# A four-head attention layer: its 65-column matmuls emitted as one burst per head, or queued and put one by one behind other matmuls

## The chip, the cores and the metric

The kernel runs on one core of a Trainium2 chip. The metric is the device time of one execution in microseconds (us), as the median of several runs. The five engines that matter are named as in the profile: PE (matmuls) with PEld (its weight loads), DVE (elementwise work and reductions), ACT (activations), POOL (here mostly indirect transfers) and SP (it issues the plain transfers). Each engine works through its own list of instructions in the order in which the program was built.

## The reference, cut to what matters

Four graph-attention layers are applied to 32 independent batch elements of 512 nodes x 256 features, each as `x = x + layer(relu(layernorm(x)))`. Layers 0 and 1 are single-head attention layers over the adjacency mask. Layer 2, the one that the change touches, has four heads of 64 features:

```python
Wh = (h @ W).reshape(B, N, 4, 64)
s_src = einsum('bnhd,hd->bnh', Wh, a_src); s_dst = einsum('bnhd,hd->bnh', Wh, a_dst)
e = leaky_relu(s_src[:, :, None, :] + s_dst[:, None, :, :], 0.2)
e = where(mask, e, -inf)                    # mask: 512 x 512 adjacency
alpha = softmax(e, axis=2)                  # per head, over the 512 sources j
h_out = einsum('bijh,bjhd->bihd', alpha, Wh)
return elu(h_out)
```

Layer 3 is an MLP with two attentions inside, one of them without a mask, which the kernel computes by sorting. Everything is fp32.

## The kernel before, in words

A row of 512 nodes is four blocks of 128 (`NT = 4`), so one batch element is a handful of 128-row tiles and all of its state stays on chip. `fast` (line 36) does the work; `general` (line 803) is a second version that runs only if a flag says that values left a safe range, and it isn't entered in the runs here.

**Streams and the planner.** Four streams (`NS = 4`, lines 760 to 786) each carry one batch element at a time through `layer0` to `layer3`. Every stage is a Python generator. When it yields, it gives a due time, and the loop at line 770 always resumes the stream whose due time is smallest. So the planner decides nothing at run time: its due times only decide the order in which the instructions of four batch elements are laid into each engine's list. `after_us(us)` (line 60) computes a due time as the stage's own start, plus `STRETCH` (2) times the matmul time that the stage has emitted so far, plus `SLOW` (1.5) times the latency that the stage names. Stream i starts `i * LEAD` planner microseconds late; `LEAD` is 75. Some instructions are tied to their place with `keep_in_program_order`.

**PSUM.** `bank()` (line 77) gives each stream two of the eight accumulator banks, in turn.

**Layer 2** (line 452). Four projections of 268 columns (lines 455 to 467) give a tile `v` that holds, for each node block and head, 64 scaled features, a column of scales (the softmax denominator's column) and two factors. The leaky ReLU of a sum, exponentiated, is written as a maximum of two products, so an attention weight needs a single VectorE instruction, `scalar_tensor_tensor` with max and then mult by the mask (line 353). It makes a 128 x 512 block: 128 sources j by all 512 targets. `weights` (line 343) makes the four blocks of a head into one tile of 128 x 4 x 512 fp32, tag `w`, four buffers. It needs the row of the other factor on all partitions. For head 0 it comes from four transposes into a PSUM bank (line 349), for heads 1 to 3 it goes out to DRAM (`rows_out`, line 362, L369) and comes back broadcast (`spread`, line 372, L375, two buffers, so the third one waits until head 1's weights are made).

For each head, `aggregate` (line 381) is called for the four target blocks t, and inside it runs over the four source blocks j: 16 matmuls of 128 x 128 weights and 65 moving columns (64 features and the denominator), which accumulate into one bank, t outermost and j innermost:

```python
for t in range(NT):
    aggregate(p[:, t * (D + 1):(t + 1) * (D + 1)], wt, t, lambda j: v[:, j, h, :D + 1])
```

All 16 are emitted in one piece, with nothing between them, and then come the reciprocal, the product into `ya` (lines 496 to 499), and after each second head the ELU and the addition to `x` (lines 500 to 506). `begin(h + 1)` makes the weights of the next head a head early. Four normalisations of pairs of blocks end the layer (lines 508 to 510).

The other layers' matmuls are longer: 257 moving columns in the single-head aggregations, 259 and 256 in projections, 512 in the MLPs (`linear_t`). All of them go through `matmul` (line 64, recorded as L66) and all transposes through `transpose` (L70).

**SP's list** holds, for one stage of the planner after another: the row out and the three spreads of a stream in layer 2 (L369, L375), the sorted values (L614, L615) and the table (L647, L648) of another stream in layer 3, stores of results (L716) and loads of inputs (L95).

Of the kernel before, what the change touches and what calls it, by code (L numbers as in the profile page):

```python
# [8 lines left out]

# [1 line left out]

# [6 lines left out]
FP = mybir.dt.float32  # L20
BF = mybir.dt.bfloat16
I32 = mybir.dt.int32
# [13 lines left out]
def fast(ctx, tc, flag, x, adj, w0, a0, w1, a1, w2, a2, mlp1_w, mlp1_b, mlp2_w, mlp2_b,  # L36
# [7 lines left out]
    NH = a2.shape[0]  # L44
    D = F // NH
    NS = 4
    LEAD = 75.0
    SLOW = 1.5
    STRETCH = 2.0

    const = ctx.enter_context(tc.tile_pool(name="const", bufs=1))
    work = ctx.enter_context(tc.tile_pool(name="work", bufs=2))
# [7 lines left out]
    def after_us(us):  # L60

        return begun[0] + STRETCH * spent[0] / CYCLES + SLOW * us

    def matmul(p, w, x, **flags):
        spent[0] += 4 * max(x.shape[-1], P)
        nc.tensor.matmul(p, w, x, **flags)  # L66

    def transpose(p, x, i, tied=False):
        spent[0] += 2 * P
        instruction = nc.tensor.transpose(p, x, i)  # L70
        if tied:
            tc.keep_in_program_order(instruction)

    active = set()
    banks = [0]

    def bank():

        own = [turn[0], *(i for i in range(NS) if i not in active and i != turn[0])]
        banks[0] += 1  # L80
        return psum.tile([P, N], FP, tag=f"b{own[banks[0] % len(own)]}", name="b", bufs=8 // NS)
# [68 lines left out]
    a0_sb = fetch_a(a0, "W0a")  # L150
    xts = {0: load_x(0)}
    W0, _ = fetched0 = fetch_w(w0, a0_sb, "W0")
    adj_sb = work.tile([P, NT, N], I32, tag="w", name="adj", bufs=4)
    nc.sync.dma_start(adj_sb, adj.rearrange("(t p) j -> p t j", p=P))
    for b in range(1, NS):
        xts[b] = load_x(b)
# [49 lines left out]

    def setup():

        own = work.tile([P, NT, N], FP, tag="w", name="own", bufs=4)
        nc.vector.tensor_scalar(own, adj_sb, 0.0, None, op0=OP.is_gt)  # L210
        nc.gpsimd.affine_select(
            out=own, in_=own, pattern=[[P, NT], [-1, N]], base=0, channel_multiplier=1,
            compare_op=OP.not_equal, fill=1.0,
        )
        tc.keep_in_program_order(nc.vector.tensor_reduce(differ[:, 0:1], adj_sb, AX.XY, OP.min))
        nc.vector.tensor_scalar(differ[:, 0:1], differ[:, 0:1], 0.0, None, op0=OP.is_lt)
        for j in range(NT):
            turn[0] = NS - 1 - j % (NS - 1)
            p = bank()
            for t in range(NT):  # L220
                transpose(p[:, t * P:(t + 1) * P], own[:, t, j * P:(j + 1) * P], ident, j + t == 0)
            nc.scalar.copy(maskT[:, j, :], p)
        turn[0] = NS - 1
        yield
        yield from finish_w(fetched1, 0.01)


        least = small([1], "rden")
        nc.vector.tensor_reduce(least, diag, AX.X, OP.min)
        nc.vector.tensor_scalar(differ[:, 1:2], least, 0.0, None, op0=OP.is_le)  # L230
        nc.vector.tensor_copy(W2[:, :, :, :D], raw2.rearrange("p k (h d) -> p k h d", d=D))
        nc.vector.tensor_scalar_mul(A2v[:, :, 1:2], A2v[:, :, 0:1], -0.8)
        nc.vector.tensor_scalar_mul(A2v[:, :, 2:3], A2v[:, :, 2:3], 0.8)
        for k in range(KF):
            project(W2[:, k, :, D:], lambda k, f: raw2[:, k, f * P:(f + 1) * P], k, A2)
            yield
        yield from finish_w(fetched3, 0.2)

        for tri, sign in ((before, 1), (after, -1)):
            nc.vector.memset(tri, 1.0)  # L240
            nc.gpsimd.affine_select(
                out=tri, in_=tri, pattern=[[sign, P]], base=0, channel_multiplier=-sign,
                compare_op=OP.is_gt, fill=0.0,
            )
        ties = work.tile([P, 2 * N - P], FP, tag="w", name="ties", bufs=4)
        nc.vector.memset(ties, TINY)
        nc.gpsimd.affine_select(
            out=ties, in_=ties, pattern=[[-1, 2 * N - P]], base=N - P, channel_multiplier=1,
            compare_op=OP.is_gt, fill=0.0,
        )  # L250
        nc.vector.tensor_copy(band, ties)
        yield
        yield from finish_w(fetched4, 0.2)
# [49 lines left out]
    def note(e):  # L303

        c = next(noted)
        nc.vector.tensor_reduce(seen[:, c:c + 1], e, AX.XY, OP.max)
# [33 lines left out]
            yield after_us(0.9 if f == ft - 1 else 0)  # L340
        return o

    def weights(r_col, t_col, masked=True, r=None):

        landed = r is not None
        if not landed:
            r = bank()
            for t in range(NT):
                transpose(r[:, t * P:(t + 1) * P], r_col(t).to_broadcast([P, P]), ident)
        wt = work.tile([P, NT, N], FP, tag="w", name="w", bufs=4)  # L350
        for j in range(NT):
            if masked:
                w = nc.vector.scalar_tensor_tensor(  # L353
                    wt[:, j, :], r, t_col(j), maskT[:, j, :], op0=OP.max, op1=OP.mult
                )
                if landed and j == 0:
                    tc.keep_in_program_order(w)
            else:
                nc.vector.tensor_scalar(wt[:, j, :], r, t_col(j), None, op0=OP.max)
        return wt  # L360

    def rows_out(cols, n):

        p = bank()
        transpose(p[:NT * n, :P], cols, ident)
        row = work.tile([P, P], FP, tag="row", name="row", bufs=1)[:NT * n, :]
        nc.scalar.copy(row, p[:NT * n, :P])
        row_d = dram.tile([n, N], FP, tag="row", name="row", bufs=4)
        nc.sync.dma_start(row_d.rearrange("n (t p) -> t n p", p=P), row)  # L369
        return row_d  # L370
# [9 lines left out]

    def aggregate(p, wt, t, rhs):
        for j in range(NT):
            matmul(p, wt[:, j, t * P:(t + 1) * P], rhs(j), start=(j == 0), stop=(j == NT - 1))

    def reciprocal(den):
        r = small([1], "rden") if len(den.shape) == 2 else small([NH, 1], "rden4")
# [65 lines left out]
    def layer2(xt, xn, rs, when):  # L452
        hT = yield from turned(xn, when)
        v = work.tile([P, NT, NH, CH], FP, tag="v", name="v2", bufs=4)
        for t in range(NT):
            ps = bank()
            for k in range(KF):
                matmul(
                    ps[:, :NH * CH], hT[:, k, t * P:(t + 1) * P], W2[:, k, :, :], start=(k == 0), stop=(k == KF - 1)
                )  # L460
            pv = ps[:, :NH * CH].rearrange("p (h c) -> p h c", c=CH)
            nc.scalar.activation(v[:, t, :, D:], pv[:, :, D:], AF.Exp, scale=rs[:, t:t + 1])
            nc.vector.scalar_tensor_tensor(  # L463
                v[:, t, :, :D], pv[:, :, :D], rs[:, t:t + 1], v[:, t, :, D:D + 1].to_broadcast([P, NH, D]),
                op0=OP.mult, op1=OP.mult,
            )
            yield after_us(0 if t + 1 < NT else 1)
        ya = work.tile([P, NT, F], FP, tag="y4", name="y4", bufs=1)
        wts = []

        def begin(h):
            wts.append(
                weights(
                    lambda t: v[:, t, h, D + 2:D + 3], lambda j: v[:, j, h, D + 1:D + 2], r=far[h]
                )
            )
            return after_us(3.2)

        row_d = rows_out(v[:, :, :, D + 2], NH)
        far = [spread(row_d[h, :]) if h else None for h in range(NH)]
        when = begin(0)
        note(v.rearrange("p t h c -> p (t h) c")[:, :, D:])
        yield after_us(3)
        for h in range(NH):
            last = when
            if h + 1 < NH:
                when = begin(h + 1)
            yield last  # L490
            wt = wts[h]
            p = bank()
            for t in range(NT):
                aggregate(p[:, t * (D + 1):(t + 1) * (D + 1)], wt, t, lambda j: v[:, j, h, :D + 1])
            pv = p[:, :NT * (D + 1)].rearrange("p (t c) -> p t c", c=D + 1)
            r = reciprocal(pv[:, :, D:])
            nc.vector.tensor_tensor(
                ya[:, :, h * D:(h + 1) * D], pv[:, :, :D], r.to_broadcast([P, NT, D]), op=OP.mult
            )
            if h % 2:  # L500
                c = slice((h - 1) * D, (h + 1) * D)
                y = ya[:, :, c]
                q = pair("q").rearrange("p a (b f) -> p (a b) f", f=2 * D)
                nc.scalar.activation(q, y, AF.Exp)  # L504
                nc.scalar.activation(y, y, AF.Relu)  # L505
                add_elu(xt[:, :, c], y, q)
            yield after_us(0)
        xn, rs = new_xn(), small([NT], "rs")
        for t0 in range(0, NT, 2):
            norm(xt, xn, rs, t0, False)  # L510
        yield after_us(7)
        return xn, rs, after_us(2)
# [720 lines left out]
```

## Time and profile before

| what | value |
|---|---|
| median of 3 runs | 2932.55 us (2931.43 to 2941.0) |
| profiled execution: its span | 2929.6 us (the page states no other time for it) |
| busy: PE / PEld / DVE / ACT / POOL | 98% / 80% / 76% / 52% / 17% of the span |
| matmul records, 65 columns | 4096, mean busy 273 ns |
| matmul records, 257 columns | 3104, mean busy 382 ns |
| DVE weight blocks (L353), 128 x 512 | 896, mean 742 to 744 ns |
| one round of four batch elements, from the repeating chain | about 355 us |

How to read it: the program holds half as many matmuls as the trace has records, because each fp32 matmul runs as two passes over the array, each with its own weight load. A transpose is one pass. Matmuls are pipelined, so the busy time of one record (273 ns) is longer than its distance to the next record's start; what counts on PE is the distance from start to start. PE's records stand in time order, and the timeline merges neighbours of the same line, shape and names.

### The profile page before, as it was taken

The page shows a single profiled execution, that of the slowest core. Times are in us where ns is not written, and L with a number is a line of the kernel's source. Part 1 is how long each engine was busy: PE and PEld are TensorE (multiplying, and loading weights), DVE is VectorE, ACT ScalarE, POOL GpSimd, SP SyncE. Part 2 cuts the span into 40 slices and gives each one's busy share as a digit, 9 for nine tenths or more (in the row PEclk, how much of TensorE's full clock was granted, in tenths as well). Part 3 has the DMA queues.
Part 4 walks back from the last instruction along what each step waited for, and adds up shares of the span by engine and source line. Part 5 has one row for each costly group of instructions (what it writes and reads, how often), then busy time and mean ns, then how long its engine had stood idle before and what let it go on. Part 6 is the DMA issues. An engine that isn't in the chain of part 4 may idle for free.

```text
span 2929.6 us, 43083 instructions
## 1 busy us (share of the span) xinstructions
PE 2858.9 (98%) x15177; PEld 2329.5 (80%) x15177; DVE 2219.9 (76%) x5676; ACT 1536.8 (52%) x3922; POOL 502.3 (17%) x515
## 2 busy tenths in 40 slices
PE   8999999999999999999999999999999999999998
PEld 6777887877888877888877888788887788877876
DVE  4677877778778778778778777787787787777764
ACT  4444455555555555555554556545555555555444
POOL 0011112112122111122021121111221111211220
PEclk9999999999999999999999999999999999999999
DMA  3033223233223333233332233222332322323230
GB/s 94 19 102 102 80 88 116 91 98 95 88 94 106 93 100 98 84 102 96 100 102 80 89 115 93 91 97 91 94 116 80 102 93 88 104 93 96 90 107 30
DMA packets 193182, 270.89 MB, mean 92 GB/s; under 512 B 17024, under 2 KB 156094, under 8 KB 192960
## 3 DMA queue, kind: packets, MB, share of 16 engines
q1 hardware_dynamic: 163200, 169.76, 18.5%
q0 software_dynamic: 29760, 98.30, 10.4%
q8 instruction: 123, 2.02, 0.3%
q14 instruction: 99, 0.81, 0.1%
HBM read 152.62 MB, written 115.39 MB: 91 GB/s over the span
## 4 chain that ended last, share of the span: by engine, by line
PE 82%; DVE 10%; ACT 4%; DMA 3%; issue 1%; SPq 0%; POOL 0%; DVEq 0%; POOLq 0%; ACTq 0%
PE b L66 75%; PE b L70 7%; DVE st L269 2%; DMA g<-table,at 2%; DVE sums L641 1%; DVE xn L280 1%; DVE x L406 1%; DVE y L405 1%; ACT v L325 1%; DVE sums L632 1%; ACT y L505 1%; ACT q L504 1%; DVE w L353 1%; ACT hT L290 1%; DVE tot L646 0%
## 5 line engine op out<-in xcount | busy, mean ns | idle before, releaser
L66 PE MATMUL b<-v,w 128*128 128x65 f32 (+1 forms) x7232 | 1218.0, 321 | 10.6 <-DVE w L353 10.5
L66 PEld LDWEIGHTS b<-v,w 128*128 128x128 f32 x7232 | 1050.0, 191 | 168.7 <-issue 56.1
L66 PE MATMUL b<-WFC,oT 128*128 128x256 f32 (+1 forms) x2048 | 495.2, 380 | 0.0
L66 PEld LDWEIGHTS b<-WFC,oT 128*128 128x128 f32 x2048 | 374.5, 189 | 49.3
L66 PE MATMUL b<-W,hT 128*128 128x259 f32 (+1 forms) x1536 | 388.8, 391 | 22.8 <-DVE v L463 14.1
L353 DVE SCALAR_TENSOR_TENSOR w<-b,v,maskT 128x512 f32<-128x512 f32 x512 | 369.4, 744 | 5.1 <-PE b L70 4.1
L607 POOL DMA_INDIRECT order<-v,at x248 | 277.0, 1117 | 490.7 <-DVE oT L730 152.3
L66 PEld LDWEIGHTS b<-W,hT 128*128 128x128 f32 x1536 | 285.3, 192 | 75.3 <-DVE v L463 17.1
L715 POOL TENSOR_TENSOR x<-x,y 128x512 f32<-128x512 f32 x62 | 87.8, 1416 | 1063.7 <-ACT y L713 950.0
L353 DVE SCALAR_TENSOR_TENSOR w<-spread,v,maskT 128x512 f32<-128x512 f32 x384 | 269.5, 742 | 0.0
L66 PE MATMUL b<-hT,WM 128*128 128x512 f32 x512 | 250.0, 599 | 0.7 <-ACT hT L290 0.7
L66 PE MATMUL b<-oT,WM 128*128 128x512 f32 x512 | 231.2, 594 | 0.0
L655 POOL DMA_INDIRECT g<-table,at x124 | 120.9, 975 | 642.8 <-ACT y L675 292.0
L387 DVE RECIPROCAL rden<-b 128x1 f32<-128x1 f32 (+1 forms) x516 | 77.3, 162 | 184.8 <-PE b L66 183.0
L529 ACT ACTIVATE v<-b,ends 128x256 f32<-128x256 f32 x256 | 118.8, 467 | 177.2 <-PE b L66 172.9
L269 DVE BATCH_NORM_STATS2 st<-x 128x6 f32<-128x256 f32 x512 | 193.3, 409 | 6.4 <-DMA x<-in_x_dram 4.1
L412 DVE TENSOR_TENSOR y<-q,y 128x512 f32<-128x512 f32 (+1 forms) x194 | 132.9, 685 | 82.9 <-ACT q L411 45.0
L339 ACT ACTIVATE oT<-b,bias 128x512 f32<-128x512 f32 x128 | 87.7, 686 | 182.7 <-PE b L66 182.0
L290 ACT ACTIVATE hT<-b 128x512 f32<-128x512 f32 x256 | 146.5, 592 | 70.3 <-PE b L70 70.2
L66 PEld LDWEIGHTS b<-oT,WM 128*128 128x128 f32 x512 | 97.5, 191 | 95.7 <-issue 92.4
L70 PE MATMUL b<-ident,xn 128*128 128x128 f32 x1024 | 147.4, 275 | 6.7 <-DVE xn L280 4.0
L70 PEld LDWEIGHTS b<-ident,xn 128*128 128x128 f32 x1024 | 123.7, 143 | 31.9 <-DVE xn L280 5.2
(143 smaller groups left out, 3748.1 us busy)
## 6 DMA issues: line engine op xcount, KB each, us to landing
table<-sums SPq DMA_DIRECT2D x62, 1032.0 KB
sums<-order SPq DMA_DIRECT2D x62, 516.0 KB
spread<-row SPq DMA_DIRECT2D x96, 256.0 KB
x<-in_x_dram SPq DMA_DIRECT2D x32, 512.0 KB
out_dram<-x SPq DMA_DIRECT2D x62, 256.0 KB
sums<-order SPq DMA_DIRECT2D x62, 129.0 KB
order<-v,at POOLq DMA_INDIRECT x248
g<-table,at POOLq DMA_INDIRECT x124
```

The lines of the kernel that those rows point to most:

```text
L66: nc.tensor.matmul(p, w, x, **flags)
L70: instruction = nc.tensor.transpose(p, x, i)
L269: nc.vector.bn_stats(st[:, i, :], xt[:, t0 + i, :])
L290: nc.scalar.activation(hT[:, :, t0 * P:(t0 + 2) * P], p.rearrange("p (k n) -> p k n", k=KF), AF.Relu)
L339: nc.scalar.activation(o[:, f, :], p, AF.Relu, bias=bias[:, f:f + 1])
L353: w = nc.vector.scalar_tensor_tensor(wt[:, j, :], r, t_col(j), maskT[:, j, :], op0=OP.max, op1=OP.mult)
L387: nc.vector.reciprocal(r, den)
L412: nc.vector.tensor_tensor(r, q, r, op=OP.add)
L529: nc.scalar.activation(halves[c][:, t, :F], ps[:, :F], AF.Copy, scale=ends[:, t, 0:1])
L607: nc.gpsimd.indirect_dma_start(out=orders[c], out_offset=bass.IndirectOffsetOnAxis(ap=at[:, 0, t:t + 1], axis=0), in_=halves[c][:, t, :], ...
L655: nc.gpsimd.indirect_dma_start(out=g, out_offset=None, in_=table, in_offset=bass.IndirectOffsetOnAxis(ap=at[:, 1, t:t + 1], axis=0),)
L715: (nc.gpsimd if n == 2 else nc.vector).tensor_tensor(xr, xr, y, op=OP.add)
```

## The change

The 65-column matmuls are no longer emitted as a burst of 16. They go into a queue (`apart`), and `matmul`, after it has emitted any matmul of at least 128 moving columns, of whichever stream, takes one from the queue and emits it right behind (`put_next`). `tc.keep_in_program_order` and `behind(..., "put")` hold them in that order. The layer-2 stage is cut accordingly: each head runs over the source blocks j outermost; for each j, one weight block is made (`AHEAD` = 3 blocks before it is used), its four matmuls (one for each t) are queued, the stage yields with a due time `PACE` = 3 planner microseconds later, and `all_put(2 * NT)` then emits whatever exceeds eight queued matmuls at once. So a head takes four due times, and the layer 16, where before there were four yields with the weight of their matmuls in them. Only the first matmul of a bank carries `start` now, where before each t region had one of its own.

A weight block is its own tile now (`[P, N]`, 16 buffers, the same memory as four whole tiles), and DVE's weight instructions of layer 2 are chained in their order (`behind(made, "weight")`). The finish of a head (reciprocal, product, ELU) moves to the third step of the next head. `ya` becomes two half-width tiles. `LEAD` goes from 75 to 79. Three setup tiles move to other tags. Numbers of matmuls, weight blocks, transposes and transfers stay the same.

```diff
-    LEAD = 75.0
+    LEAD = 79.0
+    PACE = 3.0
+    AHEAD = 3
...
+    apart = deque()
+    latest = {}
+
+    def behind(instruction, what):
+        if what in latest:
+            tc.add_manual_dep(
+                instruction.ins, latest[what].ins.name,
+                mybir.DependencyInfo(mybir.DependencyClass.NoSync, mybir.DependencyReason.DATA),
+                reason=what,
+            )
+
+    def put_next():
+        p, w, x, flags = apart.popleft()
+        instruction = nc.tensor.matmul(p, w, x, **flags)
+        tc.keep_in_program_order(instruction)
+        behind(instruction, "put")
+        latest["put"] = instruction
+
     def matmul(p, w, x, **flags):
         spent[0] += 4 * max(x.shape[-1], P)
         nc.tensor.matmul(p, w, x, **flags)
+        if apart and x.shape[-1] >= P:
+            put_next()
...
+    def put_apart(p, w, x, **flags):
+        apart.append((p, w, x, flags))
+
+    def all_put(n):
+        while len(apart) > n:
+            put_next()
...
-    adj_sb = work.tile([P, NT, N], I32, tag="w", name="adj", bufs=4)
+    adj_sb = work.tile([P, NT, N], I32, tag="sums", name="adj", bufs=2)
...
-        own = work.tile([P, NT, N], FP, tag="w", name="own", bufs=4)
+        own = work.tile([P, NT, N], FP, tag="sums", name="own", bufs=2)
...
-        ties = work.tile([P, 2 * N - P], FP, tag="w", name="ties", bufs=4)
+        ties = work.tile([P, 2 * N - P], FP, tag="v", name="ties", bufs=4)
...
+    def weight(r, t, j, masked=True, tied=False):
+        w = work.tile([P, N], FP, tag="w", name="w", bufs=4 * NT)
+        if masked:
+            made = nc.vector.scalar_tensor_tensor(w, r, t, maskT[:, j, :], op0=OP.max, op1=OP.mult)
+            if tied:
+                behind(made, "weight")
+        else:
+            made = nc.vector.tensor_scalar(w, r, t, None, op0=OP.max)
+        latest["weight"] = made
+        return w
...
-            matmul(p, wt[:, j, t * P:(t + 1) * P], rhs(j), start=(j == 0), stop=(j == NT - 1))
+            matmul(p, wt[j][:, t * P:(t + 1) * P], rhs(j), start=(j == 0), stop=(j == NT - 1))
...
+        def finish(h, p):
+            pv = p[:, :NT * (D + 1)].rearrange("p (t c) -> p t c", c=D + 1)
+            r = reciprocal(pv[:, :, D:])
+            if h % 2 == 0:
+                yas.append(work.tile([P, NT, 2 * D], FP, tag="y4", name="y4", bufs=2))
...
+        row_d = rows_out(v[:, :, :, D + 2], NH)
+        far = [spread(row_d[h, :]) if h else row(lambda t: v[:, t, 0, D + 2:D + 3]) for h in range(NH)]
+        note(v.rearrange("p t h c -> p (t h) c")[:, :, D:])
+        yield after_us(2)
+
+        def blocks():
+            for h in range(NH):
+                for j in range(NT):
+                    yield weight(far[h], v[:, j, h, D + 1:D + 2], j, True, True)
+
+        coming = blocks()
+        made = deque(next(coming) for _ in range(AHEAD))
+        ahead = None
+        for h in range(NH):
+            p = bank()
+            for j in range(NT):
+                made.append(next(coming, None))
+                w = made.popleft()
+                for t in range(NT):
+                    put_apart(
+                        p[:, t * (D + 1):(t + 1) * (D + 1)], w[:, t * P:(t + 1) * P], v[:, j, h, :D + 1],
+                        start=(j + t == 0), stop=(j + t == 2 * NT - 2),
+                    )
+                yield begun[0] + PACE
+                all_put(2 * NT)
+                if ahead is not None and j == 2:
+                    finish(*ahead)
+            ahead = h, p
+        all_put(0)
+        finish(*ahead)
```

More of the change, by code (lines that the diff above doesn't have):

```diff
@@ L12 @@
+from collections import deque
 from contextlib import ExitStack
@@ L341, in linear_t, with row, weights @@
         return o
[L343 to L360, printed above, removed]
+    def weight(r, t, j, masked=True, tied=False):
[8 more added lines that the diff above has]
+        return w
+    def row(r_col):
+        r = bank()
+        for t in range(NT):
+            transpose(r[:, t * P:(t + 1) * P], r_col(t).to_broadcast([P, P]), ident)
+        return r
+    def weights(r_col, t_col, masked=True):
+        r = row(r_col)
+        return [weight(r, t_col(j), j, masked) for j in range(NT)]
     def rows_out(cols, n):
@@ L467, in layer2 @@
             yield after_us(0 if t + 1 < NT else 1)
[L468 to L494, printed above, removed]
+        yas = []
+        def finish(h, p):
             pv = p[:, :NT * (D + 1)].rearrange("p (t c) -> p t c", c=D + 1)
             r = reciprocal(pv[:, :, D:])
-            nc.vector.tensor_tensor(
-                ya[:, :, h * D:(h + 1) * D], pv[:, :, :D], r.to_broadcast([P, NT, D]), op=OP.mult
-            )
+            if h % 2 == 0:
+                yas.append(work.tile([P, NT, 2 * D], FP, tag="y4", name="y4", bufs=2))
+            y = yas[-1]
+            c = h % 2 * D
+            nc.vector.tensor_tensor(y[:, :, c:c + D], pv[:, :, :D], r.to_broadcast([P, NT, D]), op=OP.mult)
             if h % 2:
                 c = slice((h - 1) * D, (h + 1) * D)
-                y = ya[:, :, c]
                 q = pair("q").rearrange("p a (b f) -> p (a b) f", f=2 * D)
@@ L506, in layer2 @@
                 add_elu(xt[:, :, c], y, q)
-            yield after_us(0)
+        row_d = rows_out(v[:, :, :, D + 2], NH)
[14 more added lines that the diff above has]
+                w = made.popleft()
+                for t in range(NT):
+                    put_apart(
[9 more added lines that the diff above has]
+        finish(*ahead)
         xn, rs = new_xn(), small([NT], "rs")
```

## The prediction, made before the changed kernel ran

> **What bounds the kernel now.** I read the page's busy shares first, then the chain that ended last.
>
> ```profile
> PE 2858.9 (98%) x15177; PEld 2329.5 (80%) x15177; DVE 2219.9 (76%) x5676; ACT 1536.8 (52%) x3922; POOL 502.3 (17%) x515
> ...
> PE 82%; DVE 10%; ACT 4%; DMA 3%; issue 1%; SPq 0%; POOL 0%; DVEq 0%; POOLq 0%; ACTq 0%
> PE b L66 75%; PE b L70 7%; DVE st L269 2%; DMA g<-table,at 2%; DVE sums L641 1%; DVE xn L280 1%; DVE x L406 1%; DVE y L405 1%; ACT v L325 1%; DVE sums L632 1%; ACT y L505 1%; ACT q L504 1%; DVE w L353 1%; ACT hT L290 1%; DVE tot L646 0%
> ```
>
> PE is occupied nearly throughout and carries 82% of the chain. A busy PE need not be a PE at its peak, so next I asked for the groups with their shapes kept apart, and for the timeline.
>
> ```profile
> L66 PE MATMUL b<-v,w 128*128 128x257 f32 x3104 | 756.0, 382 | 9.6 <-DVE w L353 9.5
> L66 PE MATMUL b<-v,w 128*128 128x65 f32 x4096 | 476.2, 273 | 1.0 <-DVE w L353 1.0
> ```
>
> Only 1 us was idle just before the 65-column passes, so they don't wait for data. What paces them shows in a stretch where one head's 32 passes stand between a run of 512-column passes and transposes:
>
> ```profile
> 953.81 1.45 PE L66 MATMUL b<-oT,WM 128*128 128x512 f32 x3
> 955.10 3.68 PE L66 MATMUL b<-v,w 128*128 128x65 f32 x32
> 958.61 0.61 PE L70 MATMUL b<-ident,xn 128*128 128x128 f32 x4
> ```
>
> From start to start, three 512-column passes took 1.29 us, 0.43 us each, or 0.84 ns a column. At that rate 65 columns would stream in 55 ns. But 32 passes took 3.51 us, 110 ns each. In the records themselves the distance is 112 ns for every pass but the first, which is 57. The weight loads explain both numbers:
>
> ```profile
> 954.67 0.19 PEld L66 LDWEIGHTS b<-v,w 128*128 128x128 f32 x1 [0.24 <-DVE y L405]
> 955.10 0.64 PEld L66 LDWEIGHTS b<-v,w 128*128 128x128 f32 x5 [0.24 <-issue]
> ```
>
> The first load was issued at 954.67, as the last 512-column pass began (954.666), and was hidden under it. From then on there is one load per pass, every 112 ns, and 65 columns are too short to hide one. So the limit in a burst is the weight path, at twice the streaming time.
>
> [...]
>
> **The change, part by part.** (1) *Run starts.* What is gained is the distance of a first pass against a later one: 112 - 57 = 55 ns. Does it hold for a lone short matmul, whose second load then pushes against the next matmul's load? The trace has a few such (two passes between transposes):
>
> ```profile
> 161.90 0.39 PE L70 MATMUL b<-ident,xn 128*128 128x128 f32 x2
> 162.12 0.33 PE L66 MATMUL b<-v,w 128*128 128x65 f32 x2
> 162.29 0.39 PE L70 MATMUL b<-ident,xn 128*128 128x128 f32 x2
> 162.52 0.33 PE L66 MATMUL b<-v,w 128*128 128x65 f32 x2
> ```
>
> The two passes took 162.29 - 162.12 = 0.17 us (57 to 59, then 109 to 112 ns), where two in a burst take 0.22; the transposes behind took 0.23 instead of 0.22. Eleven such places show the same. A 257-column pass behind a short one is also in the trace 78 times: it starts 112 ns after it, and its successor 217 ns later, as usual. So the long matmul doesn't pay it back. In the order of PE's instructions the 2048 short matmuls stand in 149 runs before the change (77 of 16), and in 1824 runs after it (1761 of a single one; the rest are mostly fours that were forced out). The number of passes is the same. The gain is (1824 - 149) x 55 ns = 92 us. All of it lies on PE, which is the path.
>
> (2) *What else PE's time consists of.* Taking each pass at the usual distance of its kind (257 columns 217 ns, 259: 219, 256: 215.5, 512: 429.5, 268: 226, 258: 218, transpose 109, and 57 or 112 for 65), all passes come to 2803 us. Gaps beyond that add up to 111 us, PE starts at 6.7 us, and 8 us follow its last start: 2929 us, the span. So after the change PE's steps are 2711 us. Of the 111 us of gaps, 36 lie in the first 200 us, about 14 in the last 130, and some 61 in the steady part, 8 us in each round of 355 us.
>
> (3) *The cover of the waits.* Round time falls by 11 to 12 us, to about 343. DVE has 277.7 us of work in a round (the windows' sum for one of 355 us), 78% now and 81% then. It is still no bound. But waits are covered by what the planner lays between them, and by its due times a batch element now takes 4 x 79 = 316 planner us instead of 300: layer 2's sixteen steps of 3 replace about 27 of matmul time and some waits. A planner us was worth 355/300 = 1.18 us and is then worth 343/316 = 1.09. So each named latency gets 8% less cover. Example: `after_us(7)` at the end of layer 2 falls from 12.4 to 11.4 us, for a chain of finish, ELU and four normalisations that is some 8 us of DVE and ACT work by its rows, without queueing. The cost is unknown from here: bounded by -10 us, if the even mix closes gaps (v L463 now costs 14.1), and +61, a doubling of the steady gaps. I take +20, which includes the ramp: three starts later by 4 planner us each, at most 13 us, beside PE work of other streams.
>
> ```profile
> PE b L66 <- DVE v L463: 14.1, 7, 2.9
> PE b L66 <- DVE w L353: 10.5, 18, 0.9
> ```
>
> (4) *Waits for weight blocks.* Per-block tiles add waits: PE may wait for each of 16 blocks per batch element. Behind a waiting short matmul stand all streams' matmuls, and behind those the ACT and DVE work that reads their banks. A block is asked of DVE three steps ahead, 9 planner us, 9.8 us; it takes 0.74 us, and DVE has some 20% to spare. I cost it at nothing, with DVE's lead as the cover. The count of blocks is unchanged, 16 x 0.74 us.
>
> (5) *SP.* The third spread waits until head 1's last block is made: now block 7, due about 16 planner us (17 us) after the spreads. The next entry in SP's list, the sorted values of another stream (L614), is due about 30 planner us after the spreads. Before, by SP's timeline, the third spread was issued 13 us and the sorted values 21 to 26 us after the row. So nothing is late; if it were, up to 7 us more would stand before the sorted values, with DVE's tied L625 and the table behind it. Row, table, loads and stores stay where they were, give or take one place. The setup tags, the half tiles of `ya` and the later finish move no work onto PE: zero.
>
> Sum: 2929.6 - 92 + 20 = 2858 us of span. The median of the runs stands 3 us above that span, which I add: 2861 us.
>
> **Rivals.**
> - *Cover too thin.* The gain comes, and the shorter cover returns a good part: steady gaps more than double, +65 us: 2932.5 - 92 + 65 = 2905. For it: 8% on every wait, and DVE and ACT chains between layers. Against it: waits on PE are few today, 62 us in the whole list of PE's own waits, the first transfer's 6.7 us among them.
> - *No step gained.* A lone short between long passes costs 57 + 112 as between transposes, but the long one behind it starts late by as much: 2932.5 + 3 = about 2935. Against it: the 78 places above. For it: no short alone between two long matmuls is in the trace.
> - *Slower: PE waits for each block.* DVE's list holds other streams' instructions that wait for PE, so a block may come later than its three steps. If PE stood on average 0.4 us at each of 512 blocks, 205 us: 2932.5 - 92 + 205 = 3045. It decides from 92/512 = 0.18 us a block. Against it: 9.8 us of lead.
>
> **How the numbers follow.** The forecast (gaps between -10 and +61, 2830 to 2902) has 0.66, the thin cover 0.18, no step gained 0.06, waiting for blocks 0.10. A measurement can tell about 0.3%, 9 us, from no change. Faster: 0.66 + 0.18 = 0.84; same 0.06; slower 0.10. The range takes in the first two cases, from 2830 to 2920.
>
> **What would show it.** Two passes of a lone short between 257-column passes taking 0.17 us in the timeline, and the round near 343 to 346 us, would show (1). PE's waits on w, or gaps above 111 us, show (3) and (4); L614 further behind the row than 33 us would show (5). I'm wrong if long passes behind a short one start more than 112 ns after it, or if PE's waits on w exceed some 90 us.

## The result, and the profile after

The changed kernel takes 3147.61 us (median of 4 runs, 3139.51 to 3155.15), against 2932.27 us for the kernel before in the same runs: ratio 1.0723, 95% interval 1.0697 to 1.0749. The profiled execution's span is 3137.8 us. The forecast was 2861 us, faster.

The page's busy shares and the chain that ended last, of the changed kernel:

```profile
PE 2940.5 (94%) x15177; PEld 2370.0 (76%) x15177; DVE 2209.9 (70%) x5676; ACT 1562.0 (50%) x3922; POOL 493.7 (16%) x515
...
PE 57%; DVE 20%; DMA 14%; ACT 5%; issue 3%; POOL 1%; SPq 0%; POOLq 0%; DVEq 0%; ACTq 0%
PE b L89 43%; PE b L81 8%; PE b L95 6%; DVE w L380 3%; DMA spread<-row 3%; DMA sums<-order 3%; DVE st L302 3%; DMA row<-row 2%; DMA g<-table,at 2%; DMA order<-v,at 1%; DVE xn L313 1%; DMA out_dram<-x 1%; DVE sums L687 1%; DVE sums L684 1%; DMA table<-sums 1%
```

The counts are the same as before, and in the traces PE ran the short passes in 149 runs before the change and 1824 after it, as the built order has them. PE is still the busiest engine, but its share of the chain fell from 82% to 57%. DVE and transfers took its place (34% together, 13% before): `spread` and `sums<-order` are in it now.

The short passes (now L81) and the 257-column passes, with their shapes apart:

```profile
L89 PE MATMUL b<-v,w 128*128 128x257 f32 x3104 | 834.9, 395 | 36.1 <-DVE w L380 17.4 <-ACT y L476 17.2 <-DVE w L384 0.9
L81 PE MATMUL b<-v,w 128*128 128x65 f32 x4096 | 663.0, 253 | 0.0
```

The busy total of the short passes even rises, though no more of them run. The records overlap (the first one below lasts 275 ns, and the next opens 112 ns after it), so the starts in the changed kernel's timeline have to say what they cost, in a stretch where they alternate with 257-column matmuls:

```profile
1609.81 0.39 PE L81 MATMUL b<-v,w 128*128 128x65 f32 x2
1610.03 0.65 PE L89 MATMUL b<-v,w 128*128 128x257 f32 x2
1610.52 0.33 PE L81 MATMUL b<-v,w 128*128 128x65 f32 x2
1610.69 0.65 PE L89 MATMUL b<-v,w 128*128 128x257 f32 x2
1611.18 0.33 PE L81 MATMUL b<-v,w 128*128 128x65 f32 x2
1611.34 0.65 PE L89 MATMUL b<-v,w 128*128 128x257 f32 x2
1611.83 0.33 PE L81 MATMUL b<-v,w 128*128 128x65 f32 x2
1612.00 0.43 PE L89 MATMUL b<-v,w 128*128 128x257 f32 x1
```

From 1610.69 to 1611.34 one long and one short matmul took 0.65 us. A long one behind a long one takes 2 x 217 = 434 ns, a short one inside a burst 2 x 112 = 224, together 658. So nothing is gained. The short one's two passes do take 0.16 to 0.17 us (1611.18 to 1611.34), as forecast. The long one behind it takes 0.49 us instead of 0.43. In the records its first pass stands 272 ns ahead of the second instead of 217 (medians), and this holds for all kinds: 502 passes of 257 columns, 796 of 259 (273 ns), 217 of 256 (271) and 126 of 512 columns (484 instead of 429). That is 1641 x 55 ns = 90 us, the forecast gain.

That explains a gain of zero, not a loss of 208 us of span. For the loss I counted as in the prediction. PE's passes at their usual distances come to 2713 us, and the gaps beyond them to 407 us, against 2803 and 111 before. Of the 407, 90 are the returned 55s (5 before), so some 210 us more are left. PE's own list of waits accounts for 122 of them: it adds up to 184 us, against 62 before.

Some 60 us more are passes at a lower clock. The granted clock is one half in 35 stretches of 3.4 to 10.2 us of this trace, 156 us together (5 stretches, 27 us before), so its mean is 0.975 (before 0.996). In these stretches 257-column passes start 428 ns apart instead of 217, and passes with no wait behind them took 70 us more than their usual distances (10 before). 33 of the 35 begin within 5.3 us of the start of a wait of PE of 1.4 us or more, of which this trace has 50; whether the waits bring them on is not tested.

The list of PE's waits is scattered: its longest entries are 34 us (xn L313), 27 (v L352) and 24 us (v L358). No single wait stands out on PE. On DVE some do. First the sorted values in the kernel before, then DVE's two longest waits for transfers in the changed kernel:

```profile
DVE sums L627 <- DMA sums<-order: 28.8, 28, 3.2
```

```profile
DVE sums L670 <- DMA sums<-order: 217.2, 61, 11.5
...
DVE w L380 <- DMA spread<-row: 125.0, 32, 7.0
```

(columns: us in total, times, longest us.) For these two transfers DVE stood 29 us before and 342 us after, and nothing behind them on DVE went on meanwhile (idle for 6.27 us at the place below). One such place in DVE's timeline of the changed kernel:

```profile
1578.70 0.16 DVE L633 CAST at<-found 128x4 uint32<-128x4 f32 x1
...
1597.14 0.43 DVE L670 TENSOR_TENSOR sums<-sums 128x258 f32<-128x258 f32 x1 [6.27 <-DMA sums<-order]
1597.60 0.43 DVE L671 TENSOR_TENSOR sums<-sums 128x258 f32<-128x258 f32 x1
1599.70 0.43 DVE L670 TENSOR_TENSOR sums<-sums 128x258 f32<-128x258 f32 x1 [0.65 <-DMA sums<-order]
```

At 1578.70 DVE writes the positions; POOL scatters eight blocks by them, SP reads the result back, and the addition L670 needs it, 18 us later. DVE came to L670 too soon and stood 6.27 us. Why too soon is seen in DVE's instruction list, with no time in it: the addition stands 41 places behind the positions before the change and 19 after it (medians over the batch elements). The first weight block that needs a spread stands 26 places behind layer 2's last projection before the change, and 6 after it (13 or 14 in fourteen of the 32 elements). In time, DVE was through with what stands ahead of the addition 19.1 us after the positions before the change and 13.0 us after it (medians), and the values were there at some 18 us.

### The profile page after: what moved, and what is told of

The parts are those of the page before. It is cut to its first block, busy times and chain, and to the rows that moved or that the text cites. A ratio compares the mean times of both kernels' runs of the same rounds, so it can differ in the third digit from the quotient of the medians.

```text
span 3137.8 us, 43181 instructions
## 1 busy us (share of the span) xinstructions
PE 2940.5 (94%) x15177; PEld 2370.0 (76%) x15177; DVE 2209.9 (70%) x5676; ACT 1562.0 (50%) x3922; POOL 493.7 (16%) x515
## 4 chain that ended last, share of the span: by engine, by line
PE 57%; DVE 20%; DMA 14%; ACT 5%; issue 3%; POOL 1%; SPq 0%; POOLq 0%; DVEq 0%; ACTq 0%
PE b L89 43%; PE b L81 8%; PE b L95 6%; DVE w L380 3%; DMA spread<-row 3%; DMA sums<-order 3%; DVE st L302 3%; DMA row<-row 2%; DMA g<-table,at 2%; DMA order<-v,at 1%; DVE xn L313 1%; DMA out_dram<-x 1%; DVE sums L687 1%; DVE sums L684 1%; DMA table<-sums 1%
## 5 line engine op out<-in xcount | busy, mean ns | idle before, releaser
L81 PEld LDWEIGHTS b<-v,w 128*128 128x128 f32 x4096 | 754.7, 194 | 172.9 <-issue 74.6
L89 PE MATMUL b<-v,w 128*128 128x257 f32 (+1 forms) x3136 | 841.7, 395 | 36.1 <-DVE w L380 17.4
L81 PE MATMUL b<-v,w 128*128 128x65 f32 x4096 | 663.0, 253 | 0.0
L89 PEld LDWEIGHTS b<-v,w 128*128 128x128 f32 x3136 | 555.9, 193 | 110.6 <-ACT y L476 20.7
L89 PE MATMUL b<-WFC,oT 128*128 128x256 f32 (+1 forms) x2048 | 594.2, 401 | 0.1
L89 PE MATMUL b<-W,hT 128*128 128x259 f32 (+1 forms) x1536 | 454.4, 408 | 42.5 <-ACT v L358 24.1
L89 PEld LDWEIGHTS b<-WFC,oT 128*128 128x128 f32 x2048 | 346.9, 194 | 27.9 <-issue 3.8
L89 PEld LDWEIGHTS b<-W,hT 128*128 128x128 f32 x1536 | 264.4, 195 | 96.0 <-ACT v L358 35.9
L89 PE MATMUL b<-oT,WM 128*128 128x512 f32 x512 | 257.1, 607 | 8.1 <-DVE oT L773 8.1
L89 PE MATMUL b<-hT,WM 128*128 128x512 f32 x512 | 254.8, 620 | 10.4 <-ACT hT L323 10.2
L670 DVE TENSOR_TENSOR sums<-sums 128x258 f32<-128x258 f32 x62 | 26.5, 428 | 217.4 <-DMA sums<-order 217.2
L305 ACT ACTIVATE rs<-mv,eps 128x2 f32<-128x2 f32 x256 | 74.1, 293 | 201.2 <-DVE mv L303 190.2
```

Of the source, the lines that this page charges most:

```text
L81: instruction = nc.tensor.matmul(p, w, x, **flags)
L305: nc.scalar.activation(rp, mv[:, :, 1], AF.Ln, bias=eps)
```

## The experiments

The theory formed from this is that the short matmuls' interleaving is worth nothing, and that the loss comes from layer 2's planned length. Sixteen due times of `PACE` = 3 hold 48 planner us for matmuls that took 27 before. What the planner lays beside other stages' transfers is counted in planner us, and so holds fewer instructions; the builder also moves untied instructions ahead (L670 isn't tied; L668, which the program emits just before it, is). The main rival is that interleaving itself couples all streams to each weight block. "Ties" below are `keep_in_program_order` calls. Each run's ratio is to the kernel before on the same chip. The last column gives places in DVE's list, counted in the traces as above, as medians over the batch elements. The expectations name other figures in places, above all for the first spread block (12, 16 and 15 for the changed kernel, with ties and with more cover); over all batch elements the medians are the table's.

| run | median us | ratio, 95% interval | DVE's wait for sums / spread, us | place of the addition / of the first spread block |
|---|---|---|---|---|
| before | 2932 to 2935 | 1 | 29 / 0 | 41 / 26 |
| changed | 3147.61 | 1.0723, 1.0697 to 1.0749 | 217 / 125 | 19 / 6 |
| changed, bursts of four | 3156.39 | 1.0754, 1.0734 to 1.0773 | 211 / 147 | 19 / 9 |
| changed, PACE 1.7 | 2948.05 | 1.0051, 1.0034 to 1.0068 | 56 / 0 | 47 / 30 |
| changed, PACE 1.7, bursts | 2940.1 | 1.0020, 1.0009 to 1.0032 | 65 / 0 | 38 / 30 |
| changed, PACE 1.7, ties | 2954.95 | 1.0073, 1.0056 to 1.0089 | 0 / 0 | 70 / 30 |
| changed, more cover | 3098.2 | 1.0553, 1.0531 to 1.0576 | 150 / 46 | 23 / 11 |
| changed, ties | 3080.35 | 1.0504, 1.0481 to 1.0527 | 5 / 101 | 30 / 6 |
| changed, ties, more cover | 3028.46 | 1.0331, 1.0304 to 1.0358 | 0 / 49 | 45 / 11 |
| before, longer layer 2 | 3117.68 | 1.0629, 1.0612 to 1.0646 | 160 / 106 | 32 / 10 |
| before, less cover | 3032.68 | 1.0331, 1.0294 to 1.0367 | 28 / 2 | 30 / 21 |
| before, tie | 2933.75 | 0.9996, 0.9986 to 1.0006 | 0 / 0 | 69 / 26 |
| before, interleaving | 3113.18 | 1.0615, 1.0594 to 1.0636 | 169 / 0 | 34 / 26 |
| before, interleaving, tie | 3086.85 | 1.0515, 1.0494 to 1.0536 | 0 / 0 | 69 / 26 |
| before, interleaving, tie, late finish | 3063.22 | 1.0443, 1.0420 to 1.0465 | 0 / 0 | 69 / 26 |
| changed, PACE 1.7, behind transposes | 2997.45 | 1.0227, 1.0206 to 1.0248 | 122 / 0 | 36 / 30 |

The place alone doesn't tell the wait: at 30 to 36 places DVE stood between 5 and 169 us. The time that DVE needs from the positions to the addition goes with it better: 13.0 us in the changed kernel (217 us of standing), 16.3 with the longer layer 2 (160), 18.5 with less cover (28) and 19.8 with ties (5), as medians.

**The interleaving taken away.**

```diff
 def matmul(p, w, x, **flags):
...
-        if apart and x.shape[-1] >= P:
-            put_next()
...
-                yield begun[0] + PACE
-                all_put(2 * NT)
+                all_put(0)
+                yield begun[0] + PACE
```

> The changed kernel, but each weight block's four short matmuls are emitted at once, behind nothing in particular; due times, quarter tiles and j outermost stay. Theory (the interleaving is worth nothing, since the long pass behind a short one gives the 55 ns back; the loss comes from the layer's 16 due times, which leave less TensorE work between a transfer and the VectorE instruction that needs it): as slow as the changed kernel, 3100 to 3170 us. Rival (the interleaving itself costs, by coupling all streams to each weight block): most of the loss goes, 2930 to 2980 us. If the interleaving did gain its 92 us and something else lost 300: 3230 us.

It took 3156 us, as the theory expected. The rival of coupling falls for the changed kernel: without the interleaving it is as slow.

**Layer 2's planned length in the changed kernel.** `PACE = 1.7` and `LEAD = 75.0`, nothing else.

> The changed kernel with PACE 1.7 instead of 3 and LEAD 75 instead of 79, so that layer 2 takes about as many planner microseconds as in the kernel before; the interleaving stays, though more of the short matmuls are forced out in groups (636 runs, 435 of them single). Theory (thin cover): 2930 to 2980 us. Rival (interleaving costs): about a quarter of the singles are left, so something between, 2980 to 3050 us. A third, that weight blocks per quarter tile cost by their waits: unchanged, 3100 us or more.

It took 2948 us. Two numbers of the planner bring the loss from 7.2% down to 0.5%, with quarter tiles, j outermost and 435 single short matmuls still there. DVE's two waits for transfers are down to 56 us.

**The same in the kernel before.** Layer 2 alone is stretched; no instruction is changed.

```diff
-    LEAD = 75.0
+    LEAD = 79.0
...
                 add_elu(xt[:, :, c], y, q)
-            yield after_us(0)
+            yield after_us(6)
```

> The kernel before with layer 2 stretched in the planner alone: after_us(6) instead of 0 behind each head and LEAD 79, so that a batch element takes 317 planner us as in the changed kernel; bursts, whole tiles and t outermost stay. 35 instead of 41 VectorE instructions then stand ahead of the first addition, and 11 instead of 25 ahead of the first block that needs a spread. Theory (the planned length of layer 2 is what costs): VectorE stands on the spreads for about 100 us, and the time is 2990 to 3120 us. Rival (the loss belongs to the changed instructions, not to the planned length): 2930 to 2960 us.

It took 3118 us, 87% of the loss (0.0629 of 0.0723), from due times alone. DVE's waits for transfers in this run:

```profile
DVE sums L627 <- DMA sums<-order: 160.0, 62, 6.1
DVE w L353 <- DMA spread<-row: 105.6, 31, 5.1
```

These are the changed kernel's two waits, in a kernel that has none of its instructions. With the run before this one it shows that layer 2's due times are enough to make the loss and to undo most of it. `LEAD` went with the layer's length in both runs; none parts the two.

**How much of it is DVE's standing on transfers.** First more cover by due times:

```diff
-    LEAD = 79.0
+    LEAD = 82.75
...
-        yield after_us(2)
+        yield after_us(5)
...
-        sort = after_us(11)
+        sort = after_us(18)
```

> The changed kernel with two waits given more cover: the first weight blocks are due after_us(5) instead of 2 behind the spreads' issue, and the sums after_us(18) instead of 11 behind the sorted values; LEAD follows the longer period (82.75). Theory (VectorE stands on two transfers, spread 125 us and sorted values 217 us, and all else is late behind it): these two waits fall below 60 us together and the time to 2960 to 3030 us; what is left is the thinner cover of all other waits. Rival (interleaving or quarter tiles cost): 3100 us or more, with the two waits gone all the same.

This missed: it took 3098 us, with 196 us of the two waits left. The due time moved only what is tied. The builder still drew L670 ahead, to 23 instructions behind the positions. So the ties came next, without and with that cover:

```diff
             if tied:
                 behind(made, "weight")
+                if j == 0:
+                    tc.keep_in_program_order(made)
...
-            nc.vector.tensor_tensor(sums[:, 2, 0, :], u[:, 0, :], u[:, 1, :], op=OP.add)
+            tc.keep_in_program_order(
+                nc.vector.tensor_tensor(sums[:, 2, 0, :], u[:, 0, :], u[:, 1, :], op=OP.add)
+            )
```

> The changed kernel, with two VectorE instructions kept in program order: the first weight block of each head, as it was in the kernel before, and the first addition behind the sorted values. In VectorE's list 30 instead of 19 instructions then stand between the positions (at) and the first addition, and 16 instead of 12 between the last projection and the first block that needs a spread. Theory (VectorE stands on transfers that were started too few instructions ahead): the waits for the two transfers fall from 342 us to 150 to 220, the time to 3030 to 3090 us. Rival (all waits are thinner alike): the same waits vanish, and the time stays above 3110 us.

> As the changed kernel with more cover (after_us(5) and after_us(18), LEAD 82.75), with both ties added: 45 instructions to the first addition, 15 to the first spread block. Theory: the wait for the sorted values goes below 30 us, that for the spreads to about 40, and the time to 2990 to 3050 us; what stays is the length of layer 2. Rival: both waits go and the time stays near 3098 us, as with more cover alone.

Both times are within what the theory expected: 3080 and 3028 us. Of the waits, the ties alone left 106 us, less than expected; they move no due time, and the time fell by 67 us. The wait for the sorted values went from 217 us to 5, and with the cover the spreads' from 125 to 49. With both waits down from 342 to 49 us the time fell by 119 us, some 55% of the loss; due times moved too, so the share isn't exact. The other 95 us against the kernel before are not taken apart.

**The suspect put into the kernel before.** `sort = after_us(4)` instead of 11.

> The kernel before with one number changed: the sums are due after_us(4) instead of 11 behind the sorted values. 30 instead of 41 VectorE instructions then stand between the positions and the first addition; nothing of the change is in it. Theory: VectorE stands on the sorted values for 100 to 200 us in all, and the time goes to 2990 to 3090 us. Rival (this wait is hidden, as VectorE has a quarter of its time to spare): 2930 to 2950 us.

The time, 3033 us, is in the theory's range, but not for its reason: DVE stood only 28 us on the sorted values. Its waits for PE rose instead, those at L387 from 183 to 318 us. The shorter period no longer fits `LEAD`, so I suppose that the streams' phases moved too; that isn't tested. This run tells nothing about the suspect.

**The tie alone in the kernel before, and in the changed kernel with PACE 1.7.**

> The kernel before, with the first addition behind the sorted values kept in program order, nothing else. It stands 69 instead of 41 VectorE instructions behind the positions. Theory: the 28.8 us for which VectorE stood on the sorted values vanish; TensorE is the bound and little of that reached it, so 0 to 12 us less than before. Rival: the addition and what follows it now come later than needed, and the time rises by up to 20 us.

> The changed kernel with PACE 1.7, LEAD 75 and both ties (first weight block of a head, first addition): 70 instructions ahead of the addition, 26 ahead of the first spread block. Theory: the 56 us of VectorE's wait for the sorted values that the run with PACE 1.7 still had vanish, and the time goes from 2948 to 2930 to 2945 us, no faster than the kernel before, since a lone short matmul gains nothing. If lone short matmuls did gain, below 2925 us.

In the kernel before, the 29 us of waiting vanish and the time stays (ratio 0.9996): at that level the wait is hidden. In the other the waits vanish and the time is not lower, 2955 against 2948 us, which misses the range. So taking away waits of DVE of this size, 29 and 56 us in all, gains nothing.

**Interleaving or not, at the short length.** The two edits of the first and second experiment together.

> The changed kernel with PACE 1.7 and LEAD 75, and each weight block's four short matmuls emitted at once: the run with PACE 1.7 without its interleaving. Theory (interleaving is worth nothing either way): within 0.7% of that run's 2948 us, 2930 to 2970 us. If a run's start is worth 55 ns, slower by what the fewer runs cost (636 runs there against about 450 to 500 here, some 10 us); if interleaving couples the streams, faster by 20 us or more.

2940 us, 0.3% less than with interleaving (the intervals 1.0009 to 1.0032 and 1.0034 to 1.0068 just miss each other). A burst is, if anything, the better order.

**Interleaving alone, in the kernel before.** Whole-head tiles and due times stay.

```diff
             for t in range(NT):
-                aggregate(p[:, t * (D + 1):(t + 1) * (D + 1)], wt, t, lambda j: v[:, j, h, :D + 1])
+                for j in range(NT):
+                    spent[0] += 4 * P
+                    apart.append((
+                        p[:, t * (D + 1):(t + 1) * (D + 1)], wt[:, j, t * P:(t + 1) * P], v[:, j, h, :D + 1],
+                        dict(start=(j == 0), stop=(j == NT - 1)),
+                    ))
+            yield after_us(0)
+            all_put()
...
-            yield after_us(0)
```

> The kernel before, with its whole-head weights, t outermost and its due times, but the 16 short matmuls of a head are queued, put one by one behind long matmuls until the head's due time, and the rest at once (694 runs, 529 of them single, against 149). Theory (a lone short matmul gains nothing and costs nothing): within 0.7% of the kernel before, 2920 to 2950 us. If run starts were worth 55 ns each: 545 x 0.055 = 30 us less, 2900 us. Rival (interleaving costs by coupling): 2990 us or more.

> The kernel before with the interleaving alone (as in the run of that name), and the first addition behind the sorted values kept in program order: 71 instructions ahead of it instead of 34. Theory (interleaving is free, and that run lost its time on this wait of VectorE): 2935 to 2980 us. Rival (interleaving with whole-head tiles costs of its own): above 3050 us, with the wait for the sorted values below 40 us.

> The kernel before with the interleaving alone and the tied addition, and each head's finish emitted one head later, as the changed kernel has it in its way. Theory (in that run VectorE stood 245 us on the short matmuls at the finish, since these are put late and the finish comes right behind): these waits fall below 120 us and the time from 3087 to 2950 to 3010 us. Rival (whole-head weight tiles, held a head longer, are what costs): above 3060 us.

The first misses the theory: 3113 us. With the tie the wait for the sorted values (169 us) is gone, but the time is still 3087 us. In that run DVE stood on the short matmuls (L70 there) at the heads' finish:

```profile
DVE rden L409 <- PE b L70: 245.4, 113, 5.0
```

Emitting each finish a head later left this wait at 257 us and the time at 3063 us, so neither theory's numbers came. What interleaving costs on whole-head tiles (4.4% at the least) stays open. It isn't the changed kernel's loss, which is there without interleaving.

**Short matmuls behind transposes.** `put_next` is called by `transpose` instead of `matmul`.

> The changed kernel with PACE 1.7 and LEAD 75, but a queued short matmul is put behind a transpose instead of behind a long matmul. 301 short matmuls then stand directly ahead of a transpose (49 in the run with PACE 1.7 and bursts), 252 of them between two. Theory ([...] a transpose's load is short, as the eleven places of the trace before suggest): 252 x 0.045 = 11 us less than the 2940 us of that run, so 2925 to 2935 us, at or just below the kernel before. Rival (a lone short matmul gains nothing anywhere): 2940 us or more.

The time misses, at 2997 us. DVE stood 122 us on the sorted values in it, against 65 in the run with bursts; that this made the loss is not tested. But the step is there. The timeline of this run:

```profile
252.13 0.28 PE L93 MATMUL b<-ident,xn 128*128 128x128 f32 x1
252.25 0.33 PE L81 MATMUL b<-v,w 128*128 128x65 f32 x2
252.42 0.28 PE L93 MATMUL b<-ident,xn 128*128 128x128 f32 x1
252.53 0.33 PE L81 MATMUL b<-v,w 128*128 128x65 f32 x2
252.70 0.28 PE L93 MATMUL b<-ident,xn 128*128 128x128 f32 x1
```

A transpose and a short matmul take 0.28 to 0.29 us together (252.42 to 252.70; median 286 ns at the 252 places between two transposes), where 109 + 224 = 333 would be the sum. Between transposes a lone short matmul gains 47 ns; between long matmuls it gained nothing (0.65 us for the pair, with 658 ns as the sum).

No version here beats the kernel before.

## Why the prediction was wrong, point by point

Two steps failed: (1), which made the gain, and (3), which put the loss at +20 us.

**Step (1), the run starts, failed.** "So the long matmul doesn't pay it back" is wrong: it pays back all of it, 55 ns, 1641 times. The observation under it was false. I wrote that behind those 78 long passes the successor comes "217 ns later, as usual". Counted for these 78 alone, in the trace before, it is 272 ns. 217 is the median over all 257-column passes, of which 78 of 3104 can't move it. The transposes that I showed as a model do gain, and were the wrong model. What the distances show is that a short pass took 112 ns wherever it stood, ahead of a long or a short one, once the whole period is counted (0.65 us for a long and a short matmul, where 2 x 217 + 2 x 112 = 658). Between transposes it cost less (286 ns with the transpose, where 333 would be the sum). Why isn't shown: a transpose's load is recorded as shorter, 143 against 191 ns, but right behind a short pass with 196 (median of 49 in the trace before). Where the gain went can be read from the records: behind a short pass the record of the next pass opens some 56 ns after its load starts (load at 1610.631, pass at 1610.687 in the changed kernel's trace), behind a long one 217 ns after (1610.742 and 1610.959). So a gain shows at a record's start, and it is taken back before the next start, 272 ns later instead of 217. The signs that I named at the passes could not tell: the two short passes took 0.17 us and the long ones started 112 ns behind, both as forecast, and there was still no gain. A whole period, one short and one long matmul, would have told.

**The rival "no step gained" was right on this**, except that the long matmul starts on time and lasts longer. Alone it gives 2935 us.

**Step (3), the cover, failed too: the direction was right, the size ten times too small, and the reason another.** I took the loss of cover as an average of 8% on every wait, worth +20 and at most +61 us. The gaps grew by some 210 us without the returned 55s. The even 8% never came: from row out to row out of layer 2 a round took 382 us (356 before), so a planner us was worth 382/316 = 1.21 us, not 1.09. What thinned was the cover at certain places: the stretch lies in layer 2's due times, and beside them stand the sort's transfers of another stream. Ahead of the addition cover fell from 41 to 19 places, ahead of the first spread block from 26 to 6. Both counts are in the built order and need no run; I had read that order for PE and SP but not for DVE. I also passed over a tie that the diff takes away: the first weight block of heads 1 to 3 was kept in program order. With that tie back (for all four heads) and the addition tied as well, the time is 3080 us. Some 95 us of the loss stay unexplained even with both waits nearly gone.

**Step (4), and the slower rival.** PE did not wait for weight blocks: 17.4 us in all, far from the 90 us that I set as the limit and from 205. The rival had the direction, not the place. The engine that stands longer is DVE, on transfers; PE's own waits, three times as long as before, are spread over many kinds.

**Step (5), SP.** The third spread was issued 18 us after the row, about as forecast. The sorted values left 45 us after the row, against 24 before, beyond the 33 us that I named as a sign of a late SP. But SP wasn't late: it waited 811 us for scatters (359 before). The sign was badly chosen, as it can't tell a late queue from a later stage.

**The rest.** The round of 343 us that step (3) started from fell with step (1). Costing the setup tags, half tiles and finish at nothing is borne out together: with PACE 1.7 and bursts they are all in, at 1.0020.

## What to carry to other kernels

Price a pass of TensorE with its successor, over a whole period that repeats, and never by the distance to the next record's start alone: here a lone short matmul's two passes took 0.17 us, as forecast, and with the long one behind it 0.65 us, which is no gain. Where the order is planned by due times, a longer stage takes cover from the stages beside it, unevenly: before running, count in the built order how many instructions stand between each transfer and its first reader in the list of the reader's engine, and weigh them by their durations. A wait on an engine that isn't the bound was harmless at 29 us in all (ratio 0.9996 without it), and part of a 7% loss at 342 us.

## What the runs showed of the hardware that was not expected

The first pass of a long matmul behind a 65-column pass stands some 55 ns further ahead of its second pass, at each width that was counted (272 for 217 ns at 257 columns, 273 for 219 at 259, 271 for 216 at 256, 484 for 429 at 512), and a 65-column matmul between transposes was 47 ns cheaper than in a burst (286 for 333 ns, with the transpose). The granted clock fell to a mean of 0.972 to 0.991 in the slow kernels that are derived from the changed one with `PACE` 3 (their profiled executions); in the kernel before it was 0.996. PE was recorded busy for 94% of the span in the changed kernel and 98% in the one before. In the changed kernel the mean clock of 0.975 hides 35 stretches of 3.4 to 10.2 us at one half, in which 257-column passes start 428 ns apart instead of 217.
